# LayerNorm statistics joined by GpSimd instead of VectorE's bn_aggr

## The chip, the cores and the metric

The kernel runs on one core of one Trainium2 chip. The metric is the device time of one execution in microseconds (us). In profiles PE is TensorE's matrix multiply, PEld its weight loads, DVE is VectorE, ACT is ScalarE, POOL is GpSimd and SP is SyncE, which here does nothing but issue DMAs. "L607" is line 607 of the kernel.

## What is computed

```python
x = x + _layernorm(attn(_layernorm(x, axis=-1), Wq, Wk, Wv, Wo), axis=-1)
x = x + _layernorm(ffn(_layernorm(x, axis=-1), weight, alpha, bias), axis=-1)

def _layernorm(x, axis=-1, eps=1e-05):
    m = jnp.mean(x, axis=axis, keepdims=True)
    v = jnp.var(x, axis=axis, keepdims=True)
    return (x - m) / jnp.sqrt(v + eps)
```

`x` is 8 x 1024 x 256 in float32. The attention has 16 query heads and 4 key/value heads of width 16, with rotated queries and keys; the feed-forward part is one 256 x 256 product with weights made ternary, plus a bias. Each row thus goes through four LayerNorms: before attention, after it, before the product, after it.

## The kernel before, in words

The rows are cut into 16 units of 512 (two per batch entry), each held as four tiles of 128 rows by 256. A unit goes through three phases: its projection (LayerNorm, transposes, q, k and v, rotation), its scores and exponentials, and its tail (output product, LayerNorms, feed-forward, store). The phases of different units overlap. While the scores of unit u run, the projection of unit u + 3 and the tail of unit u - 1 are threaded in between, at steps given by hand in the lists `P_PARTS` and `T_PARTS`. A unit's scores are four blocks (one per head group), each of eight steps, so a unit has 32 steps, some 3 us each.

A block works in two passes. In the first, matmuls `sm` (L582) give scores whose row maxima DVE takes with `tensor_reduce` (L607) straight from PSUM. The maxima become a shift: `mc` (L624) is transposed by PE into `pm` (L630), copied by ACT to `mh` (L632), split by DVE into `ml` (L639), and a pair of DMAs on SP writes it into spare rows of the stacked queries, `q_st<-ml` (L646). In the second pass, matmuls `se` (L655) give the scores less the shift, ACT takes the exponential (L671), and `av` (L691) multiplies with the values. The first `se` of a block can't start before its `q_st<-ml` has landed. The first pass runs ahead of the second, so `sm` of later blocks alternate with `se` of the current one.

float32 operands are held as a high and a low part ("split", L157 and L162)[...]. The keys of a unit take a way through memory: `kv_and_dram` writes them to `d_k`, reads them back as `k_rot`, `kt` rotates them on POOL (L297 to L299) and splits them into `ks`, four DMAs write `ks` to `dk` (L430: two for the high part, two for the low), and `stack_keys` reads them back in six DMAs into `k_st` (L481), twice the high part and once the low, for each of two groups of rows.

The order of work on PE, DVE and ACT is written by hand throughout. That of POOL is written by hand only at the beginning and at the end; in the long middle POOL and SP are put in order by a scheduler when the kernel is built. Each engine, and SP's queue, takes its instructions in that order.

The statistics come from `ln_stats` (L231): for each tile of 128 x 256 DVE runs `bn_stats` (L237), which leaves count, mean and summed squared deviation of two halves of the row, then `bn_aggr` (L239), which joins the halves to mean and variance in `mv`. POOL makes the reciprocal deviation (L241, L242, the latter a power of -0.5) and the negated mean (L243) in `lnsc`; `ln_apply` (L246) applies them, on POOL in most places. `ln_stats` is called by `Project.begin` (for units from 3 on; units 0 to 2 call its parts singly), and by `stats_a`, `stats_x` and `stats_f` of `Tail`, after attention, before the product and after it. Units 0 to 14 have a `Tail` with two pairs of tiles, all on POOL; the last has a `LastTail` with four single tiles, of which only the first is on POOL and the others on DVE.

Of the kernel before, what the change touches and what calls it, by code (L numbers as in the profile page):

```python
# [8 lines left out]
F32 = mybir.dt.float32  # L9
F32R = mybir.dt.float32r  # L10
AF = mybir.ActivationFunctionType
ALU = mybir.AluOpType
# [4 lines left out]
P = 128  # L17
# [6 lines left out]
EPS = 1e-5  # L24
# [4 lines left out]
def kernel(  # L29
# [29 lines left out]
    nc = tc.nc  # L59
    B, S, D = x.shape  # L60
# [14 lines left out]
    small = ctx.enter_context(tc.tile_pool(name="small", bufs=4))  # L75
# [10 lines left out]
    def load_x(u, tag, bufs):  # L86
        b, half = divmod(u, UPB)
        t = xp.tile([P, UT, D], F32, tag=tag, name=f"{tag}_{u}", bufs=bufs)
        src = x[b, half * UQ : (half + 1) * UQ, :].rearrange("(t p) d -> p t d", p=P)
        for ts in (slice(0, 2), slice(2, 4)) if u == 0 else (slice(0, 4),):  # L90
            nc.sync.dma_start(out=t[:, ts, :], in_=src[:, ts, :])
        return t

    x_sb = {0: load_x(0, "x", 2)}
# [4 lines left out]
    mhalf = const.tile([P, 2], F32, name="mhalf")  # L99
# [128 lines left out]
        nc.scalar.copy(wt, pt)  # L228


    def ln_stats(src):  # L231

        n = src.shape[1]
        mv = small.tile([P, 2, 2], F32, tag="mv", name="mv")[:, :n]
        st = small.tile([P, 2, 6], F32, tag="bnst", name="bnst")
        for t in range(n):
            nc.vector.bn_stats(st[:, t, :], src[:, t, :])  # L237
        for t in range(n):
            nc.vector.bn_aggr(mv[:, t, :], st[:, t, :])  # L239
        sc = small.tile([P, 2, 2], F32, tag="lnsc", name="lnsc")[:, :, :n]  # L240
        nc.gpsimd.tensor_scalar(sc[:, 1, :], mv[:, :, 1], EPS, 1.0, ALU.add, ALU.mult)  # L241
        nc.gpsimd.tensor_tensor(sc[:, 1, :], sc[:, 1, :], mhalf[:, :n], ALU.pow)  # L242
        nc.gpsimd.tensor_scalar(sc[:, 0, :], mv[:, :, 0], -1.0, 0.0, ALU.mult, ALU.add)  # L243
        return mv, sc

    def ln_apply(eng, dst, src, stats):  # L246
        mv, sc = stats
        for t in range(src.shape[1]):
            if eng is nc.scalar:
                eng.activation(dst[:, t, :], src[:, t, :], AF.Identity, bias=sc[:, 0, t : t + 1])  # L250
                eng.mul(dst[:, t, :], dst[:, t, :], sc[:, 1, t : t + 1])
                continue
            eng.tensor_scalar(  # L253
                dst[:, t, :],
                src[:, t, :],
                sc[:, 0, t : t + 1] if eng is nc.gpsimd else mv[:, t, 0:1],
                sc[:, 1, t : t + 1],
                ALU.add if eng is nc.gpsimd else ALU.subtract,
                ALU.mult,
            )  # L260
# [44 lines left out]
    class Project:  # L305
# [19 lines left out]
                    for p in range(2)  # L325
                ]

        def stats(self, p):
            self.sc[p] = ln_stats(x_sb[self.u][:, 2 * p : 2 * p + 2, :])

        def norm(self, p, eng=None):
            src = x_sb[self.u][:, 2 * p : 2 * p + 2, :]
# [6 lines left out]
            split_lo(eng or self.eng, self.xs[p][1], self.xn[p], self.xs[p][0])  # L339

        def begin(self, p):
            self.stats(p)
            self.norm(p)
            self.hi(p)
            self.lo(p)
# [369 lines left out]
    class Tail:  # L715
# [85 lines left out]
            ln_apply(self.eng(p), self.on[p], self.x1[p], self.sc[p])  # L801

        def stats_a(self, p):
            self.sc[p] = ln_stats(self.a[p])
            self.add(p)

        def stats_x(self, p):
            self.sc[p] = ln_stats(self.x1[p])
            self.norm(p)
            self.split(p)  # L810

        def stats_f(self, p):
            self.sc[p] = ln_stats(self.a[p])
            self.end(p)

        def ffn(self, p):
# [459 lines left out]
```

## Time and profile before

Three runs took 1648.71, 1642.97 and 1645.67 us, median 1645.67. The profiled execution took 1642.63 us; the program's own span in it is 1640.8 us, with a mean granted TensorE clock of 0.989.

| engine | busy us | share of the span | instructions |
|---|---|---|---|
| PE | 1579.7 | 96% | 14712 |
| DVE | 1399.3 | 85% | 2049 |
| ACT | 1274.8 | 78% | 2479 |
| POOL | 835.4 | 51% | 1239 |

| wait | us in all | times |
|---|---|---|
| POOL `lnsc` L241 for DVE `mv` L239 | 395.1 | 76 |
| PEld `se` L655 for ACT `e` L671 | 302.1 | 651 |
| PEld `sm` L582 for DVE `mx` L607 | 41.9 | 127 |
| PE `se` L655 for the DMA `q_st<-ml` | 9.9 | 8 |

The ends of matmuls are modelled and matmuls overlap, so PE's 96% is not PE at its peak. A wait matters only where the waiting engine is itself what the next work waits for; idle time of POOL, for one, costs nothing as such. A group's line in the profile gives, after its name and shapes, how often it ran, its busy time, the mean length of one in ns, and the idle time of its engine just before it with what ended most of it.

### The profile page before, as it was taken

How to read it: one execution, taken by the hardware profiler on the slowest of the kernel's cores; microseconds unless marked ns; L12 is line 12 of the kernel's file. 1: busy time of each engine (PE TensorE's matmuls, PEld its weight loads, DVE VectorE, ACT ScalarE, POOL GpSimd, SP SyncE). 2: the span in 40 equal slices, each digit the busy share in tenths (PEclk: the TensorE clock that was granted, in tenths of full speed). 3: DMA queues.
4: the chain of work that ended last, by engine and by line, in shares of the span. 5: the costliest groups of instructions: out<-in, count | busy, mean ns of one | idle time of the engine just before them, and what ended most of it. 6: DMA issues, size and time to landing. Idle time of an engine off the chain costs nothing.

```text
span 1640.8 us, 37250 instructions
## 1 busy us (share of the span) xinstructions
PE 1579.7 (96%) x14712; PEld 818.5 (50%) x14712; DVE 1399.3 (85%) x2049; ACT 1274.8 (78%) x2479; POOL 835.4 (51%) x1239
## 2 busy tenths in 40 slices
PE   7999999999999999999999999999999999999997
PEld 5544455454545545454544545455454544444544
DVE  7778788889898888989889898988989888898964
ACT  4657778878787887878788787887878787877884
POOL 5532457374653737455373835547374552323363
PEclk8989999999999999999999999999999999999999
DMA  4151425125151422515133251513325151231100
GB/s 139 53 101 34 91 77 101 59 76 101 56 106 49 91 67 82 101 46 105 60 83 75 77 106 44 104 49 89 71 67 104 40 97 42 46 70 34 42 15 27
DMA packets 86079, 117.99 MB, mean 72 GB/s; under 512 B 12088, under 2 KB 50808, under 8 KB 85752
## 3 DMA queue, kind: packets, MB, share of 16 engines
q1 hardware_dynamic: 85904, 115.60, 29.9%
q8 instruction: 116, 1.90, 0.5%
q14 instruction: 59, 0.48, 0.1%
HBM read 68.65 MB, written 45.88 MB: 70 GB/s over the span
## 4 chain that ended last, share of the span: by engine, by line
PE 80%; DVE 10%; DMA 3%; ACT 2%; POOL 2%; issue 2%; SPq 1%; POOLq 0%; DVEq 0%; ACTq 0%
PE av L691 28%; PE se L655 28%; PE sm L582 9%; DVE mx L607 7%; PE pa L283 3%; PE pq L283 2%; PE pf L283 2%; PE pt_ot L267 2%; ACT e L671 2%; PE pt_xt L267 2%; PE pkv L283 2%; DMA q_st<-ml 1%; DMA k_rot<-d_k 1%; PE pm L630 1%; DMA dk<-ks 1%
## 5 line engine op out<-in xcount | busy, mean ns | idle before, releaser
L607 DVE TENSOR_REDUCE mx<-sm 128x2 f32<-128x1024 f32 (+1 forms) x1304 | 1205.3, 973 | 191.9 <-PE sm L582 174.1
L671 ACT ACTIVATE e<-se 128x512 f32<-128x512 f32 x1996 | 1058.2, 602 | 223.0 <-PE sm L582 172.4
L582 PE MATMUL sm<-k_st,q_st 64*128 64x512 f32 x2048 | 748.4, 450 | 6.9 <-DVE mx L607 3.9
L655 PE MATMUL se<-q_st,k_st 64*128 64x512 f32 x2048 | 705.5, 441 | 26.7 <-ACT e L671 14.4
L691 PE MATMUL av<-e,v_aug 128*32 128x256 f32 (+3 forms) x8608 | 607.2, 378 | 0.0
L655 PEld LDWEIGHTS se<-q_st,k_st 64*128 64x128 f32 x2048 | 324.9, 185 | 405.7 <-ACT e L671 302.1
L582 PEld LDWEIGHTS sm<-k_st,q_st 64*128 64x128 f32 x2048 | 326.1, 185 | 65.1 <-DVE mx L607 41.9
L691 PEld LDWEIGHTS av<-e,v_aug 128*32 128x32 f32 x8608 | 194.4, 108 | 211.0 <-issue 148.3
L241 POOL TENSOR_SCALAR lnsc<-mv 128x2 f32<-128x2 f32 (+1 forms) x134 | 25.8, 193 | 400.1 <-DVE mv L239 395.1
L765 POOL TENSOR_TENSOR xn<-xn,a 128x512 f32<-128x512 f32 x30 | 38.4, 1282 | 131.8 <-DMA a<-d_rec 101.2
L826 POOL TENSOR_TENSOR a<-a,bias_bc 128x512 f32<-128x512 f32 x30 | 38.6, 1287 | 108.3 <-ACT a L825 108.3
L242 POOL TENSOR_TENSOR lnsc<-lnsc,mhalf 128x2 f32<-128x2 f32 (+1 forms) x134 | 92.5, 691 | 0.9
L162 POOL TENSOR_TENSOR hl<-xn,hl 128x512 fp32r<-128x512 f32 x60 | 76.5, 1287 | 0.4
L253 POOL TENSOR_SCALAR xn<-x,lnsc 128x256 f32<-128x256 f32 x116 | 65.1, 570 | 2.2
L237 DVE BATCH_NORM_STATS2 bnst<-a 128x6 f32<-128x256 f32 x120 | 44.5, 413 | 4.6 <-POOL a L826 4.6
L297 POOL TENSOR_TENSOR t<-q_rot,sin_q_sb 128x512 f32<-128x512 f32 x31 | 39.9, 1288 | 15.5 <-ACT q_rot L439 15.4
L283 PE MATMUL pa<-woh,hl 128*128 128x256 f32 x240 | 46.2, 294 | 1.1 <-ACT e L671 1.1
L283 PE MATMUL pq<-xt,wqkvh 128*128 128x256 f32 x256 | 45.8, 303 | 0.5 <-ACT e L671 0.5
L237 DVE BATCH_NORM_STATS2 bnst<-x 128x6 f32<-128x256 f32 x124 | 45.9, 412 | 0.4 <-DMA x<-in_L_attn_x 0.4
L271 ACT CAST ot<-pt_ot 128x512 fp32r<-128x512 f32 x66 | 39.6, 601 | 4.7 <-PE pt_ot L267 4.7
L439 ACT COPY q_rot<-pq 128x512 f32<-128x512 f32 x32 | 18.8, 586 | 30.9 <-PE pq L283 30.9
L162 POOL TENSOR_TENSOR hlq<-q_rot,hlq 128x512 fp32r<-128x512 f32 x31 | 39.8, 1285 | 4.8 <-ACT hlq L159 4.5
(157 smaller groups left out, 1303.1 us busy)
## 6 DMA issues: line engine op xcount, KB each, us to landing
q_st<-dq SPq DMA_DIRECT2D x90, 256.0 KB
dq<-hlq SPq DMA_DIRECT2D x60, 256.0 KB
d_av<-avsb SPq DMA_DIRECT2D x60, 256.0 KB
x<-in_L_attn_x SPq DMA_DIRECT2D x15, 512.0 KB
xn<-d_av SPq DMA_DIRECT2D x30, 256.0 KB
a<-d_rec SPq DMA_DIRECT2D x30, 256.0 KB
xr<-in_L_attn_x SPq DMA_DIRECT2D x15, 512.0 KB
out_x<-a SPq DMA_DIRECT2D x30, 256.0 KB
```

The source lines that it names most:

```text
L162: eng.tensor_tensor(lo, src, hi.bitcast(F32), ALU.subtract)
L237: nc.vector.bn_stats(st[:, t, :], src[:, t, :])
L242: nc.gpsimd.tensor_tensor(sc[:, 1, :], sc[:, 1, :], mhalf[:, :n], ALU.pow)
L253: eng.tensor_scalar(dst[:, t, :], src[:, t, :], sc[:, 0, t : t + 1] if eng is nc.gpsimd else mv[:, t, 0:1], sc[:, 1, t : t + 1], ALU.add i ...
L267: nc.tensor.transpose(pt[:, c, t * P : (t + 1) * P], src[:, t, c * P : (c + 1) * P], ident_r)
L283: nc.tensor.matmul(out, chunk(left[i], c), chunk(right[j], c), start=(k == 0), stop=(k == len(steps) - 1),)
L297: eng.tensor_tensor(dst, x, table.unsqueeze(1).to_broadcast(list(x.shape)), ALU.mult)
L582: scores = nc.tensor.matmul(sm[0][:, part, :], queries[rows], k_st[(u // UPB) % 3][rows, r2, ch * 512 : (ch + 1) * 512], start=True, stop= ...
L607: early[0] = nc.vector.tensor_reduce(mx[i][:, a, head_and_tile(i, r2, t), lo:n], sm[0][:, lo:n, :], AX.X, ALU.max).ins
L655: nc.tensor.matmul(sc if len(queries.shape) == 2 else sc.rearrange("p (j t) -> p j t", j=G), k_st[(i // G // UPB) % 3][rows, r2, kt * P : ...
L671: nc.scalar.activation(e, sc, AF.Exp, scale=1.0 / D**0.5)
L691: nc.tensor.matmul(av_ps[0][32 * r : 32 * r + 32, lo:hi], va[:, kt, r, :], es[i * NK + kt, r // 2, r % 2][:, lo:hi], start=(kt == 0 and lo ...
```

## The change

`ln_stats` gets a second argument. Where it is POOL, the two `bn_aggr` are left out and a new function joins the halves with eight operations on POOL: the mean is half the sum of the halves' means, the variance the summed squared deviations over 256 plus the square of half the difference of the means. It is given in `begin` and, where POOL applies the statistics, in `stats_a`, `stats_x` and `stats_f`. In the beginning (units 0 to 2) and in tiles 1 to 3 of the last tail `bn_aggr` stays.

```diff
+    def join_stats(neg_mean, rstd, st):
+
+        eng, (m0, m1), (s0, s1) = nc.gpsimd, (st[:, 1, i] for i in range(2)), (
+            st[:, 2, i] for i in range(2)
+        )
+        eng.tensor_tensor(neg_mean, m0, m1, ALU.add)
+        eng.tensor_scalar(neg_mean, neg_mean, -0.5, 0.0, ALU.mult, ALU.add)
+        eng.tensor_tensor(s0, s0, s1, ALU.add)
+        eng.tensor_scalar(s0, s0, 1.0 / D, EPS, ALU.mult, ALU.add)
+        eng.tensor_tensor(m0, m0, neg_mean, ALU.add)
+        eng.tensor_tensor(m0, m0, m0, ALU.mult)
+        eng.tensor_tensor(rstd, s0, m0, ALU.add)
+        eng.tensor_tensor(rstd, rstd, mhalf[:, : rstd.shape[1]], ALU.pow)
+
-    def ln_stats(src):
+    def ln_stats(src, joined_by=None):
 
         n = src.shape[1]
-        mv = small.tile([P, 2, 2], F32, tag="mv", name="mv")[:, :n]
         st = small.tile([P, 2, 6], F32, tag="bnst", name="bnst")
         for t in range(n):
             nc.vector.bn_stats(st[:, t, :], src[:, t, :])
+        sc = small.tile([P, 2, 2], F32, tag="lnsc", name="lnsc")[:, :, :n]
+        if joined_by is nc.gpsimd:
+            join_stats(sc[:, 0, :], sc[:, 1, :], st[:, :n].rearrange("p t (i k) -> p k i t", i=2))
+            return None, sc
+        mv = small.tile([P, 2, 2], F32, tag="mv", name="mv")[:, :n]
         for t in range(n):
             nc.vector.bn_aggr(mv[:, t, :], st[:, t, :])
-        sc = small.tile([P, 2, 2], F32, tag="lnsc", name="lnsc")[:, :, :n]
...
         def begin(self, p):
-            self.stats(p)
+            self.stats(p, nc.gpsimd)
...
         def stats_a(self, p):
-            self.sc[p] = ln_stats(self.a[p])
+            self.sc[p] = ln_stats(self.a[p], self.eng(p))
...
         def stats_x(self, p):
-            self.sc[p] = ln_stats(self.x1[p])
+            self.sc[p] = ln_stats(self.x1[p], self.eng(p))
...
         def stats_f(self, p):
-            self.sc[p] = ln_stats(self.a[p])
+            self.sc[p] = ln_stats(self.a[p], self.eng(p))
```

In the built program the order on PE is the same as before, and those on DVE and ACT too but for the `bn_aggr` that are gone. POOL's and SP's are not. Around the split of the keys, for units 4 to 15, they read (before on the left):

```
POOL before                          POOL changed
k_rot rotated (L297 to L299)         k_rot rotated
ks high (L157)                       t <- q_rot x sin
ks low (L162)                        join: the two sums of halves
t <- q_rot x sin (L297)              ks high
lnsc L241, L243                      q_rot x cos
q_rot x cos                          join: two scalings
                                     ks low

SP before                            SP changed
dk <- ks high x2, low x2             dk <- ks high x2
k_st <- dk x6                        k_st <- dk x1
q_st <- ml x2                        dk <- ks low x2
                                     k_st <- dk x5
                                     q_st <- ml x2
```

More of the change, by code (lines that the diff above doesn't have):

```diff
@@ L326, in __init__, with stats @@
                 ]
-        def stats(self, p):
-            self.sc[p] = ln_stats(x_sb[self.u][:, 2 * p : 2 * p + 2, :])
+        def stats(self, p, joined_by=None):
+            self.sc[p] = ln_stats(x_sb[self.u][:, 2 * p : 2 * p + 2, :], joined_by)
         def norm(self, p, eng=None):
```

## The prediction

> **What bounds the kernel now.** I read the page's chain of waits first, then the waits by engine, then one stage in order of time. The chain is PE:
>
> ```profile
> PE 80%; DVE 10%; DMA 3%; ACT 2%; POOL 2%; issue 2%; SPq 1%; POOLq 0%; DVEq 0%; ACTq 0%
> ```
>
> The 10% of DVE invites the hope that lighter statistics pay. But the chain listed in order of time has DVE, in each of the stages of 96 us from 277 to 1243, once: four reductions of L607, 3.56 us together, and no `mv`. Only from 1340 on do joins stand among such reductions; all `mv` on the chain is 3.6 us.
>
> The stage in order of time shows where the change reaches PE (start, us, engine, line):
>
> ```profile
> 821.96 0.41 POOL L157 TENSOR_SCALAR ks<-k_rot 128x256 fp32r<-128x256 f32 x1
> 822.39 2.37 SPq L430 DMA_DIRECT2D dk<-ks  x4
> 822.45 0.74 POOL L162 TENSOR_TENSOR ks<-k_rot,ks 128x256 fp32r<-128x256 f32 x1
> 823.13 1.28 POOL L297 TENSOR_TENSOR t<-q_rot,sin_q_sb 128x512 f32<-128x512 f32 x1
> 823.83 0.33 DVE L639 SCALAR_TENSOR_TENSOR ml<-mh,low,pm 32x128 fp32r<-32x128 f32 x1
> 825.71 3.33 SPq L481 DMA_DIRECT2D k_st<-dk  x6
> 829.14 1.42 SPq L646 DMA_DIRECT2D q_st<-ml  x2
> 831.23 0.46 PE L655 MATMUL se<-q_st,k_st 64*128 64x512 f32 x1 [0.33 <-DMA q_st<-ml]
> ```
>
> The shift `ml` is ready at 824.16, but its DMA starts at 829.14: it stands in SP's queue behind four writes of the split keys and six reads of them. The first `se` of the block needs it, and PE takes its matmuls in order. There are twelve such places (fourth block of units 1 to 12). The DMA starts this long after its `ml`: 4.26, 4.35, 5.05, 5.36, 4.32, 4.27, 4.98, 5.22, 4.77, 4.67, 4.14, 5.56 us, sum 56.95. Where it was 4.67, PE's gap is 0.06; at 5.56 it is 0.91; in all, gap = lateness - 4.64. So **SP already stands at the edge of the path**, and what is added there is paid one for one. The gaps now sum to 3.2 us.
>
> **The change, part by part.**
>
> *Joins leave DVE.* 116 joins of two tiles and 3 of one lose 235 `bn_aggr`.
>
> ```profile
> L239 DVE BATCH_NORM_AGGREGATE mv<-bnst 128x2 f32<-128x6 f32 x256 | 38.6, 173 | 0.4
> L241 POOL TENSOR_SCALAR lnsc<-mv 128x2 f32<-128x2 f32 x122 | 23.5, 193 | 376.9 <-DVE mv L239 372.3
> L298 POOL TENSOR_TENSOR k_rot<-k_rot,t2k 128x128 f32<-128x128 f32 x14 | 6.4, 460 | 1.1
> L298 POOL TENSOR_TENSOR q_rot<-q_rot,t 128x256 f32<-128x256 f32 x31 | 23.1, 745 | 0.5
> ```
>
> DVE: 38.6 x 235/256 = 35 us less busy. Its worth lies between nothing (no aggregate on the chain of the regular stages) and 17 us: the waits of PE and its weight loads on a reduction sum to 63.7 us, and of each I counted no more than the aggregates in DVE's unbroken run before it. I take 6, nearer the chain: some 0.4 us in each of 15 stages.
>
> *POOL takes them.* Eight operations for three, five more per join. No row shows a `tensor_tensor` of 128x2; the line through the two L298 rows (128 elements 460 ns, 256 elements 745) leaves 0.18 us at two elements, and L241 has 0.193. I take 0.19; above, 0.46. So 119 x 5 x 0.19 = 113 us more on POOL, 835 to 948 of 1641. Dependent operations start 0.08 us after the one before, so a join alone grows by 1.05 us, less 0.3 for the aggregates. Cover: `hl` of the first half is ready 4.7 us (high) and 4.2 us (low) before the transposes that read it, of the second 6.6 and 7.9, `xs` over 10; worked through the new order they come some 1.8 and 0.7 us later, the second half 2.5. DVE's `bn_stats` read what POOL wrote 5 us or more before. Cost nothing; without cover, 1 us at a join.
>
> Here a rule speaks against the change as such: the Trainium skill ("GPSIMD Engine Reference", engine selection) sends elementwise work of two inputs to VectorE, GpSimd being about twice as slow. Summed over engines the rows agree, 113 us for 35, and by the rule the kernel loses 78. But POOL idles 395 us for `mv` (the row of L241), so I charge only what reaches PE.
>
> *The order moves.* This is the price. In the built program POOL now does, between the rotated keys and their high half, the query's product with sin (1.28 us) and two operations of the join; SP writes the high halves (two DMAs), issues the first read, which waits for them, and only then writes the low halves, for which the third read waits. One round trip became two. From 821.87, keys rotated:
> - sin product 821.81 to 823.09, two operations at 0.13 apart, high half done 823.70 (was 822.37). Query (819.28) and `bnst` (819.16) are there, so nothing new is waited for.
> - First write 823.73, second 0.63 later, 824.36. Before, the second (823.02) let the first read start at 825.71: 2.7 us. So first read 827.05, low writes 827.43 and 828.06 (low half done 825.9).
> - The third read waits for the last write, 2.7 us (3.1 before, with four under way): 830.75. From it to `q_st<-ml` were 1.82 us: 832.6, against 829.14. **Delay 3.5 us** (3.4 to 3.9).
>
> Queued behind: `xn<-d_av`, `d_av<-avsb`, `dq<-hlq`; the next `ml` starts 17 us on and its block 9 us after that, so no more is late.
>
> Twelve places: 56.95 + 12 x 3.5 - 12 x 4.64 = 43.3 us of gaps, less 3.2 there already: **+40 us**, mean gap 3.6.
>
> *The clock after such gaps.* Busy times by stretch of 3.41 us, the grid of the granted clock:
>
> ```profile
> 60.03:63.44 3.41, 0.74 (x6) 0.41 (x6) 1.55 (x3) 0.95 (x3) 3.24 (x4) 1.00 0.11 29
> 63.44:66.85 3.41, 3.41 (x12) 2.24 (x13) 3.26 (x4) 2.82 (x6) 3.23 (x4) 0.50 0.00 0
> 66.85:70.26 3.41, 3.41 (x18) 2.79 (x16) 0.59 (x2) 1.26 (x3) 3.24 (x5) 0.50 0.00 0
> 199.96:203.37 3.41, 1.81 (x24) 1.05 (x25) 1.59 (x2) 1.31 (x3) 0.00 (x0) 1.00 0.56 189
> 203.37:206.78 3.41, 3.36 (x28) 1.44 (x28) 3.41 (x5) 3.28 (x8) 0.00 (x0) 1.00 0.05 9
> ```
>
> The first number behind the length is PE's busy time, the one before the last two the clock. Stretches in which PE was busy 0.49, 0.74, 1.40 and 1.51 us brought 0.50 for 3, 2, 1 and 1 stretches, one of 2.00 for 3; 1.62, 1.81 (half of a gap of 3.06 us) and 1.96 did not. A gap of 3.6 leaves, wherever the grid lies, a stretch with at most 3.41 - 1.8 = 1.6 us, so I count ten falls of two stretches. A step takes 3.02 us; of it PE's own work is four score pairs 0.22 apart (0.88), `av` 1.04 (34% of the chain from 600 to 720) and 14 us of projections over 32 steps (0.44): 2.36 us, 78%. At half clock a stretch then gives 0.5/0.78 = 64% and loses 1.2 us: 10 x 2 x 1.2 = **+24 us** (0 to 12 x 3 x 1.2 = 43). The rule ("TensorE: Matmul & The Clock Gate", HAM oscillation) names idle gaps over about 3.4 us as what brings the slow clock; seven of twelve gaps, lateness + 3.5 - 4.64, pass that, and the sum would be 17. In this trace gaps of 2.7 and 2.0 us within a stretch sufficed, so I follow the rows.
>
> *The end.* Around 1580 to 1593 POOL is busy without a break, now with four joins more: `a` L826 at 1593.64, on the chain, some 2.5 us later, and three joins until 1611 at 0.6: +4 (0 to 7).
>
> Sum: 40 + 24 + 4 - 6 = +62: span 1640.8 to 1703, the execution's own 1642.6 to 1705. The median 1645.67 lies 3 above it; with it **1707 us**.
>
> **Rivals.**
> - *The stall without the clock.* The falls stay away. For it: 201.56, a gap of 3.06 at full clock. 1645.7 + 40 + 4 - 6 = 1684.
> - *DVE's relief decides (faster).* The reductions come sooner, PE keeps all 17 us, and SP's delay is hidden. The point is lateness 4.64: each read must go out so soon that `q_st<-ml` isn't held longer than now. Then 1629. Against it: the four writes' round trip is seen in the trace, and two follow each other now.
> - *POOL becomes the bound.* If tiny operations take 0.46 us, five cost 1.35 more per join, `ks` comes 0.5 later, 12 x 0.5 = 6: 1713. If `hl` came 2 us after its cover in 12 stages too, 1737. Against it: 4.2 us of cover.
> - *The change isn't felt*: the order on the chip is that of the build, so this needs both effects to cancel; 1645.
>
> **Numbers.** Forecast 0.66, stall alone 0.16, POOL 0.11, faster 0.05, no change 0.02. The forecast's own range 1685 to 1730 and the stall alone down to 1680 hold eight in ten: 1680 to 1730. A difference within 0.3% (5 us) can't be told from none; slower 0.93.
>
> **What will show it.** `q_st<-ml` 7.5 to 9 us after its `ml` in twelve places; PE's wait on that DMA from 9.9 us in all to about 50; granted clock 0.5 after them; DVE busy about 1364, POOL 948, tiny operations near 190 ns; transposes not waiting for `hl`. Wrong would make me: first reads that don't wait for the high halves' landing, or PE gaps below 2 us.

## The result, and the profile after

The changed kernel took 1692.5 us (median of four runs, 1685.66 to 1695.32), the kernel before, on the same chip, 1645.1 us: ratio 1.028, 95% interval 1.0243 to 1.0316. The forecast was 1707, in a range of 1680 to 1730. The profiled execution took 1691.4 us with a span of 1689.6, against 1640.8 before; the mean granted clock is 0.973, against 0.989. From `ln_apply` on, line numbers are 17 higher than before (`se` is L672 in place of L655).

Three lines of the page: the engines' busy time, the chain that ended last by engine, and the group of the scores `se` with PE's idle time before them:

```profile
PE 1591.2 (94%) x14712; PEld 820.5 (49%) x14712; DVE 1377.4 (82%) x1814; ACT 1275.9 (76%) x2479; POOL 940.4 (56%) x1834
...
PE 69%; DMA 9%; POOL 8%; DVE 8%; ACT 2%; SPq 2%; issue 2%; POOLq 0%
...
L672 PE MATMUL se<-q_st,k_st 64*128 64x512 f32 x2048 | 718.1, 449 | 63.1 <-DMA q_st<-ml 46.8
```

DVE gave up 22 us of busy time (35 predicted; the records of operations that follow each other overlap, and each of the 235 `bn_aggr` frees 0.09 us and not its length of 0.17) and POOL took 105 (940.4 - 835.4; 113 predicted). Neither is the cost. On the chain PE falls from 80% to 69%, and what comes in is DMA (3% to 9%) and POOL (2% to 8%): the way of the keys through memory. The last row says where PE meets it: its wait on `q_st<-ml` went from 9.9 us to 46.8; 35.7 of that lies in the twelve places of the prediction (3.2 before), the rest in units 0 and 1.

The tiny operations of the join are not what is slow (operation, shapes, count, busy us, mean ns of one, idle time before):

```profile
L238 POOL TENSOR_TENSOR bnst<-bnst 128x2 f32<-128x2 f32 x116 | 22.9, 198 | 0.0
...
L236 POOL TENSOR_TENSOR lnsc<-bnst 128x2 f32<-128x2 f32 x116 | 22.7, 196 | 307.3 <-DVE bnst L250 307.2
...
L237 POOL TENSOR_SCALAR lnsc<-lnsc 128x2 f32<-128x2 f32 x116 | 22.2, 191 | 0.2
```

The second row shows POOL still idle for 307 us ahead of the joins; before it idled 372 for `mv`.

One of the twelve stages, a typical one (the fourth block of unit 2), in order of time (start, us, engine, line):

```profile
345.87 0.46 POOL L316 TENSOR_TENSOR k_rot<-k_rot,t2k 128x128 f32<-128x128 f32 x1
346.28 1.28 POOL L314 TENSOR_TENSOR t<-q_rot,sin_q_sb 128x512 f32<-128x512 f32 x1
347.52 0.19 POOL L236 TENSOR_TENSOR lnsc<-bnst 128x2 f32<-128x2 f32 x1
347.67 0.19 POOL L238 TENSOR_TENSOR bnst<-bnst 128x2 f32<-128x2 f32 x1
347.83 0.40 POOL L157 TENSOR_SCALAR ks<-k_rot 128x256 fp32r<-128x256 f32 x1
...
348.26 1.17 SPq L447 DMA_DIRECT2D dk<-ks  x2
348.80 0.33 DVE L656 SCALAR_TENSOR_TENSOR ml<-mh,low,pm 32x128 fp32r<-32x128 f32 x1
...
351.55 0.33 SPq L498 DMA_DIRECT2D k_st<-dk  x1
351.97 1.09 SPq L447 DMA_DIRECT2D dk<-ks  x2
353.11 3.42 SPq L498 DMA_DIRECT2D k_st<-dk  x5
356.63 1.41 SPq L663 DMA_DIRECT2D q_st<-ml  x2
358.72 0.55 PE L672 MATMUL se<-q_st,k_st 64*128 64x512 f32 x1 [2.85 <-DMA q_st<-ml]
```

The shift `ml` was ready at 349.13 (348.80 and 0.33), and its DMA went out at 356.63, 7.50 us later. Between them SP stands still twice: until 351.55 for the high halves to land, and inside the five reads, where the fourth read of all waits for the low halves. The low halves had to be written behind the first read, so the two landings follow each other. In the bracket is PE's gap, 2.85 us.

Laid end to end by the first `se` of each block, the 48.8 us of longer span divide so. In units 1 to 12 the third block, which ends with the gap, is 2.74 us longer on average (30.71 against 27.97), 32.9 in all; the fourth, which follows the gap, is 1.37 us longer (25.94 against 24.57), 16.4 in all. Everything else together is -0.5 us, in which two things nearly cancel. The first blocks of units 2 to 12 and the units from 13 on are 4.0 us shorter. The beginning, up to the second block of unit 1, is 4.0 us longer. There a gap of 2.80 us stands ahead of the third block of unit 0, where the kernel before has none. Such a gap, of 0.96 to 2.97 us, is in the traces of seven of the eight runs below too, whatever they change, so it can't be put down to the joins.

The fourth block after the gap, in four of its twelve places (window, length, PE, PEld, DVE, ACT and POOL busy, granted clock, DMA share, GB/s):

```profile
458.50:485.42 26.92, 26.43 (x233) 13.28 (x234) 21.01 (x27) 20.72 (x40) 16.49 (x31) 0.88 0.28 74
559.85:585.69 25.84, 25.35 (x233) 12.83 (x233) 21.00 (x27) 20.58 (x40) 16.00 (x31) 0.93 0.28 77
...
1165.55:1190.12 24.57, 24.08 (x234) 12.48 (x235) 20.71 (x27) 20.46 (x40) 16.44 (x31) 1.00 0.30 81
1264.48:1289.06 24.58, 24.09 (x234) 12.49 (x234) 20.73 (x27) 20.48 (x40) 16.37 (x31) 1.00 0.30 80
```

Ten of the twelve blocks have a clock under 1.00 and are 1.1 to 2.4 us longer than before; the two at 1.00, after gaps of 2.74 and 2.78 us, are as long as before. The matmuls are 233 or 234 in all four rows.

### The profile page after: what moved, and what is told of

Read it like the earlier page. It is cut to its first block, busy times and chain, and to the rows that moved or that the text cites. A ratio compares the mean times of both kernels' runs of the same rounds, so it can differ in the third digit from the quotient of the medians.

```text
span 1689.6 us, 37580 instructions
## 1 busy us (share of the span) xinstructions
PE 1591.2 (94%) x14712; PEld 820.5 (49%) x14712; DVE 1377.4 (82%) x1814; ACT 1275.9 (76%) x2479; POOL 940.4 (56%) x1834
## 4 chain that ended last, share of the span: by engine, by line
PE 69%; DMA 9%; POOL 8%; DVE 8%; ACT 2%; SPq 2%; issue 2%; POOLq 0%
PE av L708 25%; PE se L672 24%; PE sm L599 9%; DVE mx L624 6%; PE pa L300 3%; DMA q_st<-ml 2%; DMA k_rot<-d_k 2%; DMA dk<-ks 2%; PE pf L300 2%; PE pt_ot L284 2%; DMA d_k<-kv_t 2%; ACT e L688 2%; PE pkv L300 1%; PE pt_xt L284 1%; POOL t L314 1%
## 5 line engine op out<-in xcount | busy, mean ns | idle before, releaser
L672 PE MATMUL se<-q_st,k_st 64*128 64x512 f32 x2048 | 718.1, 449 | 63.1 <-DMA q_st<-ml 46.8
L599 PE MATMUL sm<-k_st,q_st 64*128 64x512 f32 x2048 | 757.6, 457 | 6.2 <-DVE mx L624 3.5
L708 PE MATMUL av<-e,v_aug 128*32 128x256 f32 (+3 forms) x8608 | 614.7, 382 | 0.0
L672 PEld LDWEIGHTS se<-q_st,k_st 64*128 64x128 f32 x2048 | 332.4, 189 | 449.9 <-ACT e L688 309.2
L599 PEld LDWEIGHTS sm<-k_st,q_st 64*128 64x128 f32 x2048 | 334.1, 189 | 60.8 <-DVE mx L624 38.3
L236 POOL TENSOR_TENSOR lnsc<-bnst 128x2 f32<-128x2 f32 (+1 forms) x119 | 23.3, 196 | 310.9 <-DVE bnst L250 310.9
L843 POOL TENSOR_TENSOR a<-a,bias_bc 128x512 f32<-128x512 f32 x30 | 38.4, 1282 | 130.9 <-ACT a L842 130.9
L243 POOL TENSOR_TENSOR lnsc<-lnsc,mhalf 128x2 f32<-128x2 f32 (+1 forms) x119 | 83.2, 700 | 9.2
L314 POOL TENSOR_TENSOR t<-q_rot,sin_q_sb 128x512 f32<-128x512 f32 x31 | 39.7, 1281 | 11.6 <-ACT q_rot L456 11.5
L721 ACT COPY avsb<-av 128x512 f32<-128x512 f32 x63 | 38.0, 603 | 5.0 <-PE av L708 4.9
```

Of the source, the lines that this page charges most:

```text
L243: eng.tensor_tensor(rstd, rstd, mhalf[:, : rstd.shape[1]], ALU.pow)
L314: eng.tensor_tensor(dst, x, table.unsqueeze(1).to_broadcast(list(x.shape)), ALU.mult)
L599: scores = nc.tensor.matmul(sm[0][:, part, :], queries[rows], k_st[(u // UPB) % 3][rows, r2, ch * 512 : (ch + 1) * 512], start=True, stop= ...
L672: nc.tensor.matmul(sc if len(queries.shape) == 2 else sc.rearrange("p (j t) -> p j t", j=G), k_st[(i // G // UPB) % 3][rows, r2, kt * P : ...
L708: nc.tensor.matmul(av_ps[0][32 * r : 32 * r + 32, lo:hi], va[:, kt, r, :], es[i * NK + kt, r // 2, r % 2][:, lo:hi], start=(kt == 0 and lo ...
```

## The experiments

All ratios are to the kernel before, run on the same chip.

### Which of the joins costs: without those of `stats_a`, and with those alone

In the built programs it is only the joins of `stats_a`, which stand ahead of the key rotation on POOL, that turn the order around the key split. So the theory can be set against a cost by the number of joins. (There are 30 such joins of two tiles; the expectations below say 29.) The first kernel is the changed one with

```diff
         def stats_a(self, p):
-            self.sc[p] = ln_stats(self.a[p], self.eng(p))
+            self.sc[p] = ln_stats(self.a[p])
```

> The changed kernel, but the joins of stats_a (29 of the 116) stay with DVE's bn_aggr; the other 87 stay with GpSimd. In this program SyncE's queue around the key split is in the order of the kernel before: four dk transfers, six k_st transfers, then q_st<-ml, with the high halves of the keys ahead of them not delayed by joins. Theory (the queue's order delays ml, and nothing else of the joins costs anything): the gaps ahead of the fourth block are as small as in the kernel before, the wait of PE on q_st<-ml about 10 us or less, the time 1640 to 1646 us. Rival (GpSimd's longer work itself costs the time, by the number of joins): three quarters of the +47 us stay, about 1680 us.

Measured: 1642.0 us, ratio 0.9978 (0.9968 to 0.9989). PE's wait on `q_st<-ml` is 11.6 us. POOL is busy 915.2 us, 80 more than before, and the time is shorter.

The second is the opposite: `stats_a` passes its engine, and `begin`, `stats_x` and `stats_f` do not.

> The kernel before, with the joins of stats_a alone (29 of the 116) given to GpSimd. SyncE's queue is in the order of the changed kernel (two dk, one k_st, two dk, five k_st, then q_st<-ml). Theory (the order decides): all or nearly all of the loss is there, 1685 to 1695 us, PE's wait on q_st<-ml 40 to 50 us. Rival (cost by the number of joins): about a quarter of +47 us, 1657 us.

Measured: 1690.9 us, ratio 1.0265 (1.0242 to 1.0289), nearly all of the loss of the changed kernel (1.028) with a quarter of its joins. POOL is busy 863.4 us. So the loss goes with the order, not with POOL's busy time: the kernel with 80 us more is no slower, the one with 28 us more is 45 us slower.

### `ml` earlier in SP's queue, all joins kept

```diff
-        (45, "x", 1, 1), (49, "kv_and_dram"), (51, "q", 0), (52, "kt"), (53, "v"), (55, "q", 1),
+        (45, "x", 1, 1), (49, "kv_and_dram"), (51, "q", 0), (54, "kt"), (53, "v"), (55, "q", 1),
```

> The changed kernel with all its 116 joins on GpSimd; only the key split (kt) is emitted two steps of the plan later (54 in place of 52). SyncE's queue then has q_st<-ml behind two dk, one k_st and one dk transfer, ahead of the last dk and five k_st transfers. Theory (ml's place in the queue): the wait of PE on q_st<-ml falls under 10 us, the granted clock stays full in units 1 to 12, the time is 1638 to 1646 us. Rival (GpSimd's work is what delays): nothing is gained, 1690 us. A third: ml is early but the k_st transfers are now late, and the wait moves to the first scores of the next unit: 1660 us or more, with q_st<-ml gone from the list of waits and k_st in it.

Measured: 1638.5 us, ratio 0.9951 (0.9935 to 0.9967), the fastest of all kernels here. The same stage as above, in order of time:

```profile
343.95 0.41 POOL L157 TENSOR_SCALAR ks<-k_rot 128x256 fp32r<-128x256 f32 x1
344.38 1.17 SPq L447 DMA_DIRECT2D dk<-ks  x2
344.90 0.33 DVE L656 SCALAR_TENSOR_TENSOR ml<-mh,low,pm 32x128 fp32r<-32x128 f32 x1
346.11 0.74 POOL L162 TENSOR_TENSOR ks<-k_rot,ks 128x256 fp32r<-128x256 f32 x1
347.67 0.32 SPq L498 DMA_DIRECT2D k_st<-dk  x1
348.09 0.52 SPq L447 DMA_DIRECT2D dk<-ks  x1
348.70 1.41 SPq L663 DMA_DIRECT2D q_st<-ml  x2
350.16 0.56 SPq L447 DMA_DIRECT2D dk<-ks  x1
350.77 0.94 SPq L498 DMA_DIRECT2D k_st<-dk  x2
```

`ml` is ready at 345.23 and goes out 3.48 us later; it stands behind one landing in place of two. The high half of the keys is as late behind their rotation as in the changed kernel (1.92 us on average in place of 0.50 before), so POOL's work is all there; only the queue is different. Of twelve gaps one is left, 1.95 us, and all twelve fourth blocks show a clock of 1.00. PE's wait on `q_st<-ml` is 12.8 us, not under 10 as expected, but 10.9 of it lie in units 0 and 1. That the reads of the keys now come last is not felt, no wait of PE on them is listed: the third expectation fails.

### DVE's relief alone

In the kernel before, `bn_aggr` is left out where the changed kernel joins on POOL:

```diff
-        for t in range(n):
-            nc.vector.bn_aggr(mv[:, t, :], st[:, t, :])
+        if left_out:
+            mv = st[:, :n, 1:3]
+        else:
...
```

> The kernel before, with bn_aggr left out wherever the changed kernel joins on GpSimd: the join of the two halves is not computed at all, mean and variance are taken from the first half, and GpSimd's three small operations stay as before. This is DVE's relief alone (116 joins, 232 bn_aggr of 173 ns, 40 us less of DVE's busy time), without the longer chain on GpSimd. Theory (the relief lies beside PE's work nearly everywhere, only the last two units feel it): 1639 to 1645 us, that is 0 to 6 us less than before. Rival (DVE decides): 1629 us or less, the relief of the stages in which the chain runs through DVE.

Measured: 1640.5 us, ratio 0.9963 (0.9950 to 0.9977), so 6 us gained (4 to 8). DVE's busy time falls from 1399.3 to 1376.5 us, POOL's stays (835.7). That is within the theory, and far from the rival. It is what a lighter DVE is worth in this kernel when nothing else moves (the mean and variance are then those of the first half of each row, which leaves the work the same).

### What turns the order: one tiny operation more, or two

Here no join is moved. In the kernel before, POOL multiplies the negated mean by 1.0, once or twice, in the `stats_a` that it applies (30 of two tiles and one of a single tile):

```diff
         nc.gpsimd.tensor_scalar(sc[:, 0, :], mv[:, :, 0], -1.0, 0.0, ALU.mult, ALU.add)
+        for _ in range(extra):
+            nc.gpsimd.tensor_scalar(sc[:, 0, :], sc[:, 0, :], 1.0, 0.0, ALU.mult, ALU.add)
...
-            self.sc[p] = ln_stats(self.a[p])
+            self.sc[p] = ln_stats(self.a[p], 1 if self.eng(p) is nc.gpsimd else 0)
```

> The kernel before, all joins on DVE as they were, with one small operation more on GpSimd (the negated mean times 1.0, 128x2, about 193 ns) in each of the 30 stats_a that GpSimd applies: 30 operations, 5.8 us more of GpSimd's busy time. The built queue of SyncE is in the order of the kernel before. Theory (only the order costs): 1644 to 1648 us, PE's wait on q_st<-ml about 10 us. Rival (each delay on GpSimd ahead of the key rotation is paid by PE in full): 12 delays of 0.19 us, about 2 us more, 1648 us.

Measured: 1649.4 us, ratio 1.0021 (1.0007 to 1.0035). The loss of 3.5 us lies above the theory's range and is no less than the rival's 2 us, but it is not in the rival's place: in the twelve places the gaps sum to 3.1 us (3.2 before), and the third and fourth blocks are as long as before. What is longer in its trace is the third block of unit 0 (2.7 us) and the second of unit 1 (2.2), as in most of the other traces. Where the small loss comes from stays open.

> The same with two such operations in each of the 30 places: 60 operations, 11.6 us more of GpSimd's busy time, DVE as in the kernel before, no join moved. The built queue of SyncE is here in the order of the changed kernel (two dk, one k_st, two dk, five k_st, then q_st<-ml). Theory (the order costs, whatever turns it): 1683 to 1693 us, PE's wait on q_st<-ml 40 to 50 us. Rival (GpSimd's time costs in proportion): twice the last run's loss at most, 1646 to 1650 us. Second rival (the joins as such are needed for the loss): 1646 us.

Measured: 1668.0 us, ratio 1.0149 (1.0127 to 1.0171). PE's wait is 27.1 us. Both rivals fall: the second operation, some 6 us of POOL's time in all, costs five times what the first does (18.6 us against 3.5). But the theory's number is missed too; only half of the changed kernel's loss is here. The stage of unit 3 shows why:

```profile
433.78 0.45 POOL L301 TENSOR_TENSOR k_rot<-k_rot,t2k 128x128 f32<-128x128 f32 x1
434.32 0.40 POOL L157 TENSOR_SCALAR ks<-k_rot 128x256 fp32r<-128x256 f32 x1
434.69 1.27 POOL L299 TENSOR_TENSOR t<-q_rot,sin_q_sb 128x512 f32<-128x512 f32 x1
434.75 1.16 SPq L432 DMA_DIRECT2D dk<-ks  x2
...
438.00 0.33 SPq L483 DMA_DIRECT2D k_st<-dk  x1
438.42 1.09 SPq L432 DMA_DIRECT2D dk<-ks  x2
439.55 3.39 SPq L483 DMA_DIRECT2D k_st<-dk  x5
443.06 1.41 SPq L648 DMA_DIRECT2D q_st<-ml  x2
```

SP's order is that of the changed kernel, but on POOL the high half of the keys follows the rotation at once; the query's product with sin comes behind it. The order of SP alone is thus seen by itself. Means over the twelve places, in us:

| kernel | keys rotated to high half done | high half done to `ml` DMA | `ml` ready to its DMA | PE's gap |
|---|---|---|---|---|
| before | 0.50 | 6.98 | 4.75 | 0.27 |
| two operations | 0.50 | 8.60 | 6.23 | 1.61 |
| joins of `stats_a` alone | 1.62 | 8.45 | 7.13 | 2.50 |
| changed | 1.91 | 8.52 | 7.61 | 2.97 |
| changed, key split later | 1.92 | 4.41 | 3.71 | 0.16 |

SP's order is worth 1.5 to 1.6 us of lateness, the product with sin ahead of the high half 1.12 (1.62 - 0.50), the two operations of the join 0.29 (1.91 - 1.62). In every row but the last, gap and lateness differ by 4.48 to 4.64, as in the prediction.

### The clock apart from the wait

Six matmuls that nothing reads are put ahead of the first `se` of the fourth block in units 1 to 12 of the changed kernel:

```diff
+        u, j = divmod(i, G)
+        if s % (4 * NK) == 0 and j == G - 1 and 1 <= u <= 12:
+            for _ in range(6):
+                nc.tensor.matmul(
+                    sc, ident_r, k_st[(u // UPB) % 3][:, 0, :UQ], start=True, stop=True
+                )
         exp_scores(n, r2, a, sc)
```

> The changed kernel, with six matmuls more that nothing reads (128 rows, 512 columns, about 0.40 us each, 2.4 us together) ahead of the first scores of the fourth block of units 1 to 12, into the bank that those scores then overwrite. The queue's order and the wait for q_st<-ml stay. Theory (of the loss, 33 us are the wait and 16 us the half clock after it): the wait's place is filled, the granted clock stays full in the fourth blocks, their mean length falls from 25.94 back to about 24.6 us, the time is 1674 to 1680 us. Rival (the longer fourth blocks are contention with the transfers that came late, not the clock): 1690 us and the fourth blocks stay at 25.9 us. Second rival (matmuls that nothing waits for do not hold the clock when they end ahead of the scores): as the first.

Measured: 1676.1 us, ratio 1.0188 (1.0168 to 1.0209), 16 us less than the changed kernel, by adding work to the busiest engine. The six took 1.68 us, less than the 2.4 expected, and a wait is left behind them:

```profile
350.41 1.68 PE L690 MATMUL se<-k_st,ident_r 128*128 128x512 f32 x6
353.26 0.50 PE L672 MATMUL se<-q_st,k_st 64*128 64x512 f32 x1 [1.17 <-DMA q_st<-ml]
```

1.68 + 1.17 us is the gap of 2.85 us again; the DMA is as late as before (7.51 us here). The fourth blocks, though, are at full clock (same columns as above):

```profile
451.94:476.63 24.69, 24.03 (x234) 12.55 (x235) 20.72 (x27) 20.45 (x40) 16.55 (x31) 1.00 0.31 81
551.14:575.80 24.66, 24.09 (x233) 12.56 (x234) 20.72 (x27) 20.47 (x40) 16.28 (x31) 1.00 0.30 81
...
850.21:876.14 25.93, 25.39 (x233) 12.99 (x234) 21.00 (x27) 20.70 (x40) 15.49 (x31) 0.93 0.29 77
```

Eleven of twelve are at 1.00; their mean, with the one that fell (it had 2.06 us of idle time left), is 24.77 us. The third blocks stay long (30.56 us). So wait and clock are two costs, 33 and 16 us in the changed kernel. Filling the wait wins back 14 of the 16 in the fourth blocks with the transfers as late as before, so contention with them is not the second cost.

### The later key split without any join

The kernel with two more operations on POOL, with `kt` at step 54:

> The kernel of the run before last (two small operations more in 30 places, all joins on DVE), with the key split emitted two steps of the plan later (54 in place of 52). SyncE's queue then has q_st<-ml behind two dk, one k_st, two dk and two k_st transfers, and ahead of the last three k_st, so ahead of the read that waits for the low halves. Theory (ml's place in the queue costs, not GpSimd's time, and the gain of the third run over the kernel before is mostly the relief of DVE): PE's wait on q_st<-ml at or under 13 us, the clock full in the fourth blocks, 1642 to 1648 us. Rival (the later key split is itself the gain of the third run): 1638 to 1641 us. Second rival (it stays behind a late transfer): 1660 us or more.

Measured: 1640.2 us, ratio 0.9969 (0.9958 to 0.9981): the rival's number. PE's wait is 10.2 us, the lateness 3.85, one gap of 0.72 us. The theory, that the third run gained mostly by DVE's relief, is wrong. So most of what the fastest kernel gains over the one before, 5 of 8 us, comes with the later key split and without a single join; what its joins add is the remaining 3 us, at the edge of what the intervals can separate. In the traces the 3.2 us of gaps in the twelve places fall to 0.7 here and to 1.95 in the third run; where the rest of the gain lies can't be read from single executions, which differ by several us (the profiled one of the kernel before lies 3 us under its median).

## Why the prediction was right, and where its sizes were off

The mechanism of the loss held in each step that the prediction named: the order of POOL and SP, two landings in series, PE's gap of lateness less 4.64, the clock after it. Both large terms were too high, and the forecast lies 14.5 us above the median. The terms, in us:

| term | predicted | shown by the trace |
|---|---|---|
| gaps in twelve places | +40 | +32.5 (sum 35.7 less 3.2) |
| clock after them | +24 | +16.4 |
| end | +4 | +2.5 (third block of the last unit) |
| DVE's relief | -6 | -6.1 in three places (-6 by the run of it alone) |
| not in the sum | 0 | +3.5 (of it +4.0 up to unit 1) |
| span | +62 | +48.8 |

**The delay.** 3.5 us was predicted, 2.87 came. The high half came 1.41 us later (1.33 predicted), and landings took 2.75 us from the second write to the first read (2.7 predicted). The term that was off is the end of the chain: the working took the third read as the one that waits for the low halves and added 1.82 us from there to `ml`. In the changed program it is the fourth (second to third read 0.55 us, third to fourth 1.66), and from there only 1.35 us are left. The order of the reads had changed as well, which the working left out. The rest of the difference is that the stage worked through had a shorter queue before than most: 6.77 us from the high half to the `ml` DMA, where the mean is 6.98.

**The clock.** Ten falls were predicted, and there were ten of twelve. That the number came out is in part luck: the working rested on gaps of 3.6 us, which leave a stretch of little work wherever they lie, and the gaps came out at 2.97, which do not (the last section has the two that differ). Each was to last two stretches of 3.41 us at 1.2 us; a stretch costs about that much (25.84 - 24.57 = 1.27 in the second row of those windows), but five of the ten falls lasted one stretch: there are 15 at half clock, not 20, for 16.4 us, 1.1 each. The rule of the Trainium skill that the prediction set aside ("TensorE: Matmul & The Clock Gate", HAM oscillation), idle gaps of over about 3.4 us, would have given fewer: only two of the twelve gaps are longer (3.86 and 4.31), and ten blocks fell. That the prediction's sum by this rule, 17 us, lies near the 16.4 is chance, since it is made of seven falls of two stretches.

**The end.** The term is there, hidden by another. The third block of unit 15 is 2.5 us longer (24.88 against 22.34): `a` L843 starts 22.1 us into it in place of 19.9, and PE then waits 1.07 us for `hl` of POOL. The other three kernels with the joins of `begin`, `stats_x` and `stats_f` on POOL have it too (1.7 to 2.6 us), the others don't. The last block is 2.4 us shorter, so the unit as a whole shows nothing.

**DVE's relief.** The total was right, its division was not, so part of that is luck: 0.4 us in each of 15 stages was assumed. In the trace of the changed kernel the first blocks of units 2 to 12, where the chain has its four reductions, are 0.20 us shorter on average, 2.2 in all. The run of the relief alone has 0.23 there, the kernel with two more operations and no relief nothing. Units 13 and 14 are 1.5 us shorter together, where reductions and joins meet on the chain, and the last block 2.4. The last block is 1.3 to 2.4 us shorter in all five kernels in which DVE is rid of the joins of `begin`, `stats_x` and `stats_f`, and in none of the others. Part of it is a stretch at half clock (at 1613 us) that the changed kernel does not have there, so that it is all relief is not shown.

**The rivals.** The stall without the clock (1684) was cheaper than what came, and the last experiment but one shows the clock's part apart; that DVE decides, or POOL is the bound, is excluded by the kernels with the joins of `stats_a` left out or alone. The rule of the Trainium skill that the prediction set aside ("GPSIMD Engine Reference", engine selection), that elementwise work of two inputs belongs on VectorE, would by the prediction's estimate from busy times have had a loss of 78 us; the first experiment has 80 us more of POOL's work for 18 us less of DVE's, and no loss. The cover ahead of the transposes held nearly: all waits of PE and its weight loads for POOL grew from 17.3 to 23.0 us, over 45 places, none longer than 1.2.

## What to carry to other kernels

When a change gives more work to an engine whose order a scheduler makes, compare the built orders of that engine and of the DMA queue it feeds before adding up durations: here two operations of 0.19 us turned the queue and cost 22 us, while 80 us of work on the same engine cost nothing. Look in each queue for the transfer that the bound engine waits for, and for what stands ahead of it that itself waits for a landing; moving the producer two steps later in the plan turned a loss of 47 us into a gain of 8. And look at the clock behind a stall of the matmul engine: here it fell in ten of twelve places and cost half as much again as the stalls themselves (16 us to 33).

## What the hardware showed that I had not expected

**The clock falls after short gaps, but not after all.** In the changed kernel a gap of 2.51 us was followed by a fall and one of 2.78 us was not. Length alone doesn't decide. The granted clock changes on a grid of 3.41 us in the traces, and the rows show the stretches of this grid around two gaps, the first of 2.85 us, the second of 2.78 (length, PE's busy time first, the clock third from the end):

```profile
355.54:358.96 3.42, 0.57 (x10) 0.27 (x4) 0.10 (x1) 0.39 (x1) 3.25 (x5) 1.00 0.20 62
358.96:362.37 3.41, 3.41 (x20) 1.42 (x18) 2.15 (x3) 1.94 (x4) 3.27 (x8) 0.50 0.26 82
...
1260.08:1263.49 3.41, 1.62 (x17) 1.01 (x16) 1.38 (x3) 0.90 (x2) 3.05 (x6) 1.00 0.34 106
1263.49:1266.91 3.42, 2.43 (x20) 1.29 (x20) 1.66 (x2) 1.75 (x4) 3.42 (x6) 1.00 0.23 63
```

The first gap lies in one stretch and leaves 0.57 us of PE's work in it; the second lies across two, which keep 1.62 and 2.43. So it is in all twelve places: the ten that fell had a stretch with 0.28 to 1.59 us of work, the two that did not have 1.62 and 1.71 at least. But the busy time of one stretch is not all either. With two more operations on POOL, a gap of 1.37 us with 2.04 us of work in its stretch was followed by half clock, and one of 1.66 us with 1.75 was not:

```profile
443.55:446.96 3.41, 2.04 (x24) 0.78 (x16) 1.25 (x4) 1.60 (x4) 3.25 (x6) 1.00 0.17 34
446.96:450.38 3.42, 3.42 (x18) 1.51 (x18) 2.65 (x4) 2.55 (x6) 3.42 (x6) 0.50 0.20 70
...
839.50:842.91 3.41, 1.75 (x19) 1.08 (x18) 1.35 (x5) 0.66 (x2) 3.41 (x4) 1.00 0.22 65
842.91:846.32 3.41, 3.41 (x32) 1.42 (x28) 3.02 (x4) 3.14 (x7) 3.25 (x6) 1.00 0.27 82
```

In the ten traces together, every stretch at full clock with under 1.59 us of PE's work was followed by half clock, none with over 2.35 was, and between the two both happened. The Trainium skill ("TensorE: Matmul & The Clock Gate", what's actually happening) says that activity is watched in a free-running window of some 3.4 us; the grid agrees with that, and what decides between 1.59 and 2.35 us no run here shows.

**A landing costs the queue, not only its reader.** From the second write of the high half to the read that waits for it SP took 2.7 to 2.8 us on average in every kernel, and everything behind that read stood still. The Trainium skill ("DMA: Bandwidth & Descriptors", anatomy of one DMA, which describes DMAs issued by GpSimd) says that a wait for a semaphore is made by the issuing sequencer, ahead of the dispatch; the stages above, whose DMAs SP issues, agree.
